# Local attention layer: taps taken in pairs, norms and reciprocals through 32x32 transposes, TensorE's order written out in nine turns

## The chip, the core and the metric

The kernel runs on one core of a Trainium2 chip. The metric is device time in microseconds (us); of a kernel's runs the median counts. Five engines work side by side, each on its own queue: TensorE (PE in the profile, its weight loads PEld) multiplies matrices into PSUM, VectorE (DVE), ScalarE (ACT) and GpSimd (POOL) work element by element, SyncE (SP) issues the DMAs. A queue is worked off in order: an instruction that waits holds up everything behind it on its engine.

## What is computed

Four residual layers, one after the other, on two images of 512 channels by 64x64 tokens, all in float32. The change is in layer 0, which is worked through once for each image. Cut to what matters:

```python
q = (xf @ W_q + b_q).reshape(B, N, nh, hd).transpose(0, 2, 1, 3)      # 8 heads of 64 channels
q_norm = _l2norm(q)
q_scaled = (q_norm + query_embedding[None]) * jax.nn.softplus(temperature)[None]
kv = xf @ W_kv + b_kv                                                 # k also divided by its norm
patches = ...                                                         # the 3x3 neighbours of a token
attn_local = jnp.einsum('bhnd,bhndk->bhnk', q_scaled, k_local)        # 9 "taps" per token and head
...
attn_pool = jnp.einsum('bhnd,bhpd->bhnp', q_scaled, _l2norm(k_pool))  # 256 pooled keys
attn = jax.nn.softmax(jnp.concatenate([attn_local, attn_pool], axis=-1), axis=-1)
a_local, a_pool = (attn[..., :ll], attn[..., ll:])
lt = jnp.einsum('bhnd,hdk->bhnk', q_norm, learnable_tokens) + learnable_bias[None] + a_local
x_local = jnp.einsum('bhnk,bhndk->bhnd', lt, v_local)
x_pool = jnp.einsum('bhnp,bhpd->bhnd', a_pool, v_pool)
out = ((x_local + x_pool).transpose(0, 2, 1, 3).reshape(B, N, C)) @ W_proj + b_proj
```

## The kernel before

**Units and turns.** Class `Local` holds the layer. Channels lie on the 128 partitions, so a chunk of 128 channels is two heads. A *unit* is one chunk with 1024 tokens (16 image rows); there are 4 chunks times 4 stretches of tokens, 16 units. The loop of `run` (from L1995) goes over *turns* i = -4 to 16, and in each turn works on several units at different stages: it projects k of unit i+4 and q of unit i+3 (and, from turn 3 on, v of unit i+1), divides the k and q that the turn before projected by their norms, makes the tap scores of unit i+1, does the softmax of unit i and weighs the values of unit i-1 with it. Turns 3 to 11 hold the same work; earlier and later ones hold less of one stage or another.

**Order.** Each stage is a Python generator. `in_turn` advances every stage by one `yield` after the other, so a turn has ten steps, and within a step the stages come in the order of the list `stages`: `norms`, `tap_products`, `attend`, `weigh`, `tap_sums`, `projections`, `normed`. This program order is where the framework starts; it then issues an engine's instructions in the order in which its own model of their durations finds them ready. That order is fixed at build time, and each engine follows it on the chip. Five of the eight PSUM banks are handed out by `bank()` to all stages, one more takes the tap sums, two take a copy of q.

**Norms.** `projections` leaves k or q of 512 tokens in SBUF (ACT, L2242) and its square in one of four tiles `sq` (ACT, L2244). A turn later `norms` multiplies four such squares by a matrix of ones (PE, L2276): the sum of squares of stream s and head r stands in row 32s + r of a bank. ACT copies the bank to `n_rows` (L2279), PE transposes it in four 128x128 pieces (L2283), so that the sums lie on tokens, and 13 small DVE operations of 32 elements (L2290 to L2298) make the inverse root: an integer first guess and three Newton rounds. The results go into `wide`, a tile of zeros, three yields later PE transposes it back (L2304) and ACT copies it (L2306). `normed` spreads each row over its 64 channels with a product (PE, L2318) and DVE multiplies k or q by it (L2326). `learned` then makes the scores of the learnable tokens (PE, L2339).

**Taps.** `tap_products` copies q into PSUM (ACT, L2361) and multiplies it by nine shifted windows of the image of k, one DVE operation of 1024 elements each (L2366), into three tiles in turn. `tap_sums` adds up the channels of each head with products of 32 columns (PE, L2379): tap k of half j goes to column group 2j + k % 2, so four of them can lie side by side in the array. ACT takes the exponential (L2394).

**Softmax.** `attend` makes the scores of the pooled keys in four pairs of products (PE, L2411) with their exponentials (ACT, L2415), multiplies them by the pooled values (PE, L2421), adds probabilities in pairs (POOL, L2426) and sums them (PE, L2433 and L2437) into a bank whose 32 rows of a group hold the two heads' denominators 16 times over, alternating. DVE takes the reciprocal of all 128x512 elements in two halves (L2458), and two more operations make the tap weights (L2461, L2462).

**Weighing.** The weights go through DRAM (SP, L2465) and come back spread over the partitions, one DMA pair for each of ten weights (`fetch_tap`, L2477), into a ring of three tiles. For each, `weigh` copies the tile into two banks (ACT, L2491), multiplies by the shifted v (DVE, L2496 and L2499) and adds to the output (POOL, L2504); when a tile is free again, the weight three further on is fetched. The sum goes to DRAM (SP, L2510). From turn 14 on `output` reads it back and multiplies by W_proj (PE, L2199), which `fetch_output` loads into the four `sq` tiles in turn 13 (L2175).

Of the kernel before, what the change touches and what calls it, by code (L numbers as in the profile page):

```python
# [3 lines left out]

# [1910 lines left out]
class Local:  # L1915
# [9 lines left out]
    def __init__(self, net, X, Y, sp_scale, d, wp, yp, pp, ppt, pps):  # L1925
        self.net, self.nc, self.vec, self.cst = net, net.nc, net.vec, net.cst
        self.X, self.Y, self.sp_scale, self.d = X, Y, sp_scale, d
        self.wp, self.pp, self.ppt, self.pps = wp, pp, ppt, pps
        nc, new = self.nc, lambda shape, name: wp.tile(shape, F32, name=name)

        self.yd = yp.tile([P, KC, N], F32, name="yd")
        self.wd = yp.tile([3, P, KC, C], F32, name="wd")
        self.rows = cycle([yp.tile([P // 2, self.UT], F32, name=f"rows{i}") for i in range(2)]).__next__

        R = W + 2
        flat = Y.rearrange("p k n -> p (k n)")
        self.next_w = flat[:, :KC * C].rearrange("p (kc o) -> p kc o", kc=KC)
        whole = Lent(flat)
        self.kx, self.vx = (whole.take([P, R, R]) for _ in range(2))
        qs, self.kraw = whole.take([P, 3 * self.UT]), whole.take([P, self.UT])  # L1940
        self.qs = [qs[:, i * self.UT:(i + 1) * self.UT] for i in range(3)]
        weighed = whole.take([P, 2 * self.UT])

        self.taps = ([weighed[:, i * self.UT:(i + 1) * self.UT] for i in range(2)]
                     + [new([P, self.UT], "tap2")])
        self.prods = [whole.take([P, self.UT])] + [new([P, self.UT], f"prod{i}") for i in range(2)]
# [19 lines left out]
        self.qn = new([P, self.UT], "qn")  # L1966
# [3 lines left out]
        self.wide = new([P, NT, P], "wide")  # L1970
# [12 lines left out]
        nc.gpsimd.memset(self.wide, 0.0)  # L1983

        nc.vector.tensor_tensor(self.qb, self.vec[:, V_QE:V_QE + KC], sp_scale, ALU.mult)

# [8 lines left out]
    def run(self):  # L1995
# [9 lines left out]
            self.fetch(i, 0)  # L2005
        for i in range(-4, units + 1):
            k, q, ahead, u, before = (unit(i + n) for n in (4, 3, 1, 0, -1))
            streams, ended = [], []
            stages = [self.norms(streams, ended)]
            if ahead is not None:  # L2010
# [4 lines left out]
                stages.append(self.weigh(before))  # L2015
            if ahead is not None:
                stages.append(self.tap_sums(ahead))

            values = ([ahead] if i >= self.UN - 1 and ahead is not None
                      else {-4: [0], -3: [1, 2], -2: [3]}.get(i, []))  # L2020
            stages.append(self.projections(k, q, values, streams))
# [4 lines left out]
                stages.append(self.fetch_output())  # L2026
            if i > units - 3:
                stages.append(self.output(i - units + 2))
            in_turn(*stages)

        self.nc.sync.dma_start(self.next_w, self.d["w_q1"].rearrange("(kc p) o -> p kc o", p=P))
        in_turn(self.output(KC - 1))
# [135 lines left out]

    def fetch_output(self):

        for _ in range(3):

            yield
        for kc in range(KC):
# [5 lines left out]
    def output(self, c4):  # L2180
# [1 line left out]

        nc, net = self.nc, self.net
        units = KC * self.UN
        toks = ([self.prods[0], self.prods[1], self.prods[2], self.qs[(units - 2) % 3]] if c4 % 2
                else [self.kraw, self.qn,
                      self.w3[:, :2].rearrange("p i k o -> p (i k o)"), self.qs[(units - 3) % 3]])
        for kc in range(KC):
# [43 lines left out]
    def projections(self, uk, uq, uvs, streams):  # L2232
# [19 lines left out]
        elif last - 1 in uvs:  # L2252

            uvs = [last - 1, last]
        values = [(u, j) for u in uvs for j in range(2)]
        for step in range(10):
            if step >= 6:
                project((uk, uq)[step // 2 - 3], "kq"[step // 2 - 3], step % 2)
            if step % 3 == 0 and values:
                u, j = values.pop(0)  # L2260
                self.value(u, j)
                if j and self.last(u):
                    self.fetch("v", u // self.UN + 1)
            yield

    def norms(self, streams, ended):
# [8 lines left out]
        for s in range(4):  # L2275
            nc.tensor.matmul(ps[32 * s:32 * s + 32, :], self.cst[:, C_E32:C_E32 + 32],  # L2276
                             before[s % len(before)][4], start=True, stop=True)
        rows = wp.tile([P, TB], F32, name="n_rows")
        nc.scalar.copy(rows, ps)  # L2279
        yield  # L2280
        ps = self.bank()
        for t in range(NT):
            nc.tensor.transpose(ps[:, t * P:(t + 1) * P], rows[:, t * P:(t + 1) * P],  # L2283
                                self.net.ident)


        sums = ps.rearrange("p (t s r) -> p t s r", t=NT, s=4)
        n, a = (sums[:, :, :, 2 * i:2 * i + 2] for i in range(2))
        y = wp.tile([P, NT, 4, 2], F32, name="roots")
# [4 lines left out]
        for i in range(3):  # L2294
            nc.vector.tensor_tensor(a, n, y, ALU.mult)
            nc.vector.tensor_tensor(a, a, y, ALU.mult)
            dst = self.wide.rearrange("p t (s r) -> p t s r", s=4)[:, :, :, :2] if i == 2 else y
            nc.vector.scalar_tensor_tensor(dst, a, 1.5, y, ALU.add, ALU.mult)  # L2298
        yield
        yield  # L2300
        yield
        ps = self.bank()
        for t in range(NT):
            nc.tensor.transpose(ps[:, t * P:(t + 1) * P], self.wide[:, t, :], self.net.ident)  # L2304
        rows = wp.tile([P, TB], F32, name="n_rows")
        nc.scalar.copy(rows, ps)  # L2306
        ended += [(s, rows[32 * s:32 * s + 2, :], *a) for s, a in enumerate(before)]
        yield

    def normed(self, ended):  # L2310

        nc = self.nc
        for _ in range(5):
            yield
        for which in "kq":
            mine = [(e, self.bank()) for e in ended if e[2] == which]
# [3 lines left out]
            for (_, _, _, u, j, part, _), ps in mine:  # L2320
                out = part
                if which == "k":
                    y = 1 + u % self.UN * self.UY + j * self.UY // 2
                    out = self.kx[:, y:y + self.UY // 2, 1:W + 1]
                    part, ps = (a.rearrange("p (y x) -> p y x", x=W) for a in (part, ps))
                nc.vector.tensor_tensor(out, part, ps, ALU.mult)  # L2326
            yield
        if mine:
            self.learned(mine[-1][0][3])
# [26 lines left out]
    def tap_products(self, u):  # L2356

        qs = self.pps.tile([P, self.UT], F32, name="qs")
        for j in range(2):
            part = slice(j * TB, (j + 1) * TB)  # L2360
            self.nc.scalar.copy(qs[:, part], self.qs[u % 3][:, part])  # L2361
        qs = qs.rearrange("p (y x) -> p y x", x=W)
        y = u % self.UN * self.UY
        for k in range(9):
            dy, dx = divmod(k, 3)
            self.nc.vector.tensor_tensor(  # L2366
                self.prods[k % 3].rearrange("p (y x) -> p y x", x=W), qs,
                self.kx[:, y + dy:y + dy + self.UY, dx:dx + W], ALU.mult)
            yield

    def tap_sums(self, u):

        nc = self.nc
        ps = self.ppt.tile([P, TB], F32, name="tap")

        def sums(k):
            for j in range(2):
                q = 2 * j + k % 2
                nc.tensor.matmul(ps[32 * q:32 * q + 32, :],  # L2379
                                 self.cst[:, C_TAPW + 16 - 2 * k:C_TAPW + 48 - 2 * k],  # L2380
                                 self.prods[k % 3][:, j * TB:(j + 1) * TB], start=(k < 2),
                                 stop=(k > 6))

        yield
        yield
        for k in range(0, 8, 2):
            sums(k)
            sums(k + 1)
            yield
            if k < 6:  # L2390
                yield
        sums(8)
        el = self.els()
        nc.scalar.activation(el, ps, AF.Exp)  # L2394
        self.el[u] = el
# [2 lines left out]
    def attend(self, u):  # L2398
# [43 lines left out]
        yield  # L2442
        exponentials(0, 1)
        yield
        values(0)
        yield
        exponentials(1, 0)
        yield
        exponentials(1, 1)
# [3 lines left out]
        yield  # L2453
        psD = sums()

        for i in range(2):
            part = slice(i * TB // 2, (i + 1) * TB // 2)
            nc.vector.reciprocal(self.recip[:, part], psD[:, part])  # L2458
# [242 lines left out]
```

## Time and profile before

| what | us |
|---|---|
| median of 3 runs (range) | 5152.03 (5151.96 to 5159.61) |
| the profiled execution's own time | 5163.61 |
| its span, first to last instruction | 5161.7 |
| TensorE busy | 4898.0 (95%) |
| VectorE busy | 3067.8 (59%) |
| ScalarE busy | 1863.1 (36%) |
| GpSimd busy | 1844.2 (36%) |
| mean granted TensorE clock | 0.979 of full speed |
| turns -3 to 0, first image | 194.6 to 326.9 |
| turns 1 and 2 | 326.9 to 419.7 |
| turns 3 to 11 | 419.7 to 818.2 |
| turns 12 and 13, then the tail with the output product | 818.2 to about 1000 |
| turns 3 to 11, second image | 2979.8 to 3378.6 |

A turn is bounded here by the first product of L2276, which every turn from -3 to 13 has. In the profile a line of instructions gives start, duration, engine, source line and operation, tiles written and read, and shape; "[2.21 <-PE mm L2318]" is idle time of the engine just before and who ended it. A matmul's duration overlaps the next one's, so what a product costs TensorE is read from start to start. A float32 product appears as two instructions.

### The profile page before, as it was taken

The numbers are of one execution on the slowest core, as the hardware profiler recorded it, in microseconds if no ns is written. First come the engines' busy times: TensorE is split into PE (matmuls) and PEld (weight loads), VectorE is DVE, ScalarE is ACT, GpSimd is POOL, SyncE is SP. The second block draws the span as 40 slices with busy tenths as digits, with TensorE's granted clock in tenths as the row PEclk, the third lists the DMA queues.
The fourth block names the chain that finished last, engine by engine and source line by source line (L and its number), as shares of the span: only waits on it lengthen the run. The fifth ranks groups of instructions, "written<-read, shape, count | busy, mean of one in ns | idle before, by whom it ended". The sixth has DMA issues, their size and how long they took to land. (4 is left out here: it accounts for less than half of the span.)

```text
span 5161.7 us, 48736 instructions
## 1 busy us (share of the span) xinstructions
PE 4898.0 (95%) x17299; PEld 2034.4 (39%) x17299; DVE 3067.8 (59%) x3986; ACT 1863.1 (36%) x3547; POOL 1844.2 (36%) x1216
## 2 busy tenths in 40 slices
PE   7999999899999999999999999998999999999998
PEld 3423332555334444433344333325543344444333
DVE  4266777644579633478732677776446795334766
ACT  1245565324323233322112555652343232333221
POOL 0035566500420045454500455555013201454554
PEclk9999999999999999999999999999999999999999
DMA  3025556600000000211110355565000000000111
GB/s 149 2 78 137 144 140 171 173 27 10 1 1 17 1 1 1 66 52 49 58 70 3 96 142 140 143 168 163 19 10 1 2 15 1 1 1 21 39 46 44
DMA packets 124752, 309.88 MB, mean 60 GB/s; under 512 B 20882, under 2 KB 33682, under 8 KB 122964
## 3 DMA queue, kind: packets, MB, share of 16 engines
q1 hardware_dynamic: 124500, 306.68, 21.0%
q8 instruction: 139, 2.28, 0.2%
q14 instruction: 113, 0.93, 0.1%
HBM read 258.11 MB, written 48.50 MB: 59 GB/s over the span
## 5 line engine op out<-in xcount | busy, mean ns | idle before, releaser
L134 PE MATMUL mm<-big,w 128*128 128x512 f32 x2496 | 1162.5, 610 | 9.2 <-DVE late L2458 9.2
L134 PEld LDWEIGHTS mm<-big,w 128*128 128x128 f32 x2496 | 455.9, 192 | 677.0 <-issue 559.0
L2504 POOL TENSOR_TENSOR late<-late,big 128x1024 f32<-128x1024 f32 x192 | 454.1, 2365 | 196.4 <-DVE big L2499 178.8
L1616 POOL TENSOR_TENSOR big<-big 128x512 f32<-128x512 f32 x224 | 277.3, 1270 | 219.8 <-ACT big L1607 219.8
L2426 POOL TENSOR_TENSOR late<-late 128x512 f32<-128x512 f32 x128 | 160.6, 1276 | 514.6 <-ACT late L2415 492.6
L2499 DVE TENSOR_TENSOR big<-big,mm 128x512 f32<-128x512 f32 x384 | 255.9, 683 | 124.5 <-ACT mm L2491 104.5
L2491 ACT COPY mm<-big 128x512 f32<-128x512 f32 x428 | 244.8, 593 | 174.0 <-DMA big<-rows 140.3
L1607 ACT ACTIVATE big<-mm,ed 128x256 f32<-128x256 f32 x512 | 193.6, 489 | 232.8 <-DVE top L1603 200.4
L2504 POOL TENSOR_TENSOR late<-late,tap 128x1024 f32<-128x1024 f32 x96 | 227.1, 2366 | 101.1 <-DVE tap L2499 97.8
L1420 POOL TENSOR_TENSOR wq<-prob 128x512 f32<-128x512 f32 x48 | 70.8, 1498 | 506.6 <-ACT prob L1417 506.6
L1871 PE MATMUL mm<-k,w 128*128 128x512 f32 x512 | 236.8, 606 | 12.3 <-DVE k L1864 7.3
L1603 DVE TENSOR_REDUCE top<-mm 128x1 f32<-128x512 f32 x256 | 159.1, 684 | 148.5 <-PE mm L1535 148.5
L134 PE MATMUL mm<-big,wq 128*128 128x512 f32 x512 | 235.2, 609 | 2.7 <-ACT off_t L1219 2.7
L2366 DVE TENSOR_TENSOR prod<-qs,big 128x1024 f32<-128x1024 f32 x192 | 230.7, 1217 | 8.7 <-PE tap L2379 7.0
L1191 PE MATMUL mm<-big,wo 128*128 128x512 f32 x512 | 234.7, 604 | 0.0
L1581 PE MATMUL mm<-w,big 128*128 128x512 f32 x512 | 234.5, 601 | 0.0
L1346 PE MATMUL acc<-big,diag 128*128 128x512 f32 x512 | 226.5, 601 | 4.6 <-ACT diag L1344 4.6
L1861 DVE RECIPROCAL psD<-psD 128x512 f32<-128x512 f32 x64 | 215.1, 3362 | 1.9
L969 POOL TENSOR_TENSOR group_stats<-group_stats,cst 128x1 f32<-128x1 f32 (+1 forms) x20 | 12.1, 621 | 570.2 <-DVE group_stats L968 538.7
L2379 PE MATMUL tap<-prod,cst 128*32 128x512 f32 x768 | 198.3, 602 | 8.9 <-DVE prod L2366 8.0
L134 PE MATMUL mm<-big,big 128*128 128x512 f32 x464 | 201.7, 594 | 0.5 <-DVE b_sr L1007 0.5
L1417 ACT ACTIVATE prob<-mm 128x512 f32<-128x512 f32 x256 | 133.0, 603 | 171.6 <-PE mm L1414 171.4
(410 smaller groups left out, 8477.2 us busy)
## 6 DMA issues: line engine op xcount, KB each, us to landing
big<-rows SPq DMA_DIRECT2D x428, 256.0 KB, 4.3
tap<-rows SPq DMA_DIRECT2D x212, 256.0 KB, 4.2
yd<-late SPq DMA_DIRECT2D x32, 512.0 KB, 2.9
lost_all<-lost SPq DMA_DIRECT2D x128, 128.0 KB, 3.1
out<-big SPq DMA_DIRECT2D x64, 256.0 KB, 2.0
big<-in_W_kv SPq DMA_DIRECT2D x8, 1024.0 KB, 9.4
rows<-late SPq DMA_DIRECT2D x64, 128.0 KB, 2.3
big<-yd SPq DMA_DIRECT2D x16, 512.0 KB, 5.1
```

Source lines behind the costliest of these rows:

```text
L134: self.nc.tensor.matmul(ps, w[:, kc, :], X[:, kc, blk * TB:(blk + 1) * TB], start=(kc == 0), stop=(kc == KC - 1))
L1191: nc.tensor.matmul(ps, w[:, kc, oc * P:(oc + 1) * P], att[:, kc, :], start=(kc == 0), stop=(kc == KC - 1))
L1346: nc.tensor.matmul(accs[b], dg, src[:, b * TB:(b + 1) * TB], start=(j == 0), stop=(j == 6))
L1581: nc.tensor.matmul(ps, X[:, kc, lo:lo + P], wv[:, kc, :], start=(kc == 0), stop=(kc == KC - 1))
L1616: nc.gpsimd.tensor_tensor(a, a, part, ALU.add)
L1861: nc.vector.reciprocal(psD, psD)
L1871: nc.tensor.matmul(ps, self.wo[:, kc, oc * P:(oc + 1) * P], qs[:, kc, :], start=(kc == 0), stop=(kc == KC - 1))
L2366: self.nc.vector.tensor_tensor(self.prods[k % 3].rearrange("p (y x) -> p y x", x=W), qs, self.kx[:, y + dy:y + dy + self.UY, dx:dx + W], A ...
L2379: nc.tensor.matmul(ps[32 * q:32 * q + 32, :], self.cst[:, C_TAPW + 16 - 2 * k:C_TAPW + 48 - 2 * k], self.prods[k % 3][:, j * TB:(j + 1) * ...
L2491: nc.scalar.copy(ps, part)
L2499: nc.vector.tensor_tensor(part.rearrange("p (y x) -> p y x", x=W), self.vx[:, y:y + self.UY // 2, dx:dx + W], ps.rearrange("p (y x) -> p y ...
L2504: nc.gpsimd.tensor_tensor(out, out, t, ALU.add)
```

## The change

- `tap_products` multiplies two taps with one operation of 2048 elements (the window of the second tap as a further dimension), and the ninth alone; the two product tiles hold two taps each, and a pair's four sums for each pass follow one another in `tap_sums`.
- `norms`: DVE transposes the bank of sums in place in blocks of 32x32, the 13 small operations work there, and a second 32x32 transpose writes the rows to `sq[3]`. Both copies by ACT and both sets of transposes by PE go, with `wide` and its clearing and with three yields.
- The reciprocal: DVE transposes the bank of denominators in place, takes the reciprocal of one of the 16 equal pairs (32 elements a partition), and transposes it, repeated 16 times, into `recip`.
- In turns 3 to 11 (`steady`) TensorE's instructions keep program order, and the steps are set anew: k is projected at steps 4 and 6, q at 7 and 8, v at 0 and 2; the norm rows are spread at steps 3 and 4; the first pooled values come one step later and in the same step as the next exponentials; the third pair of products is issued on DVE behind the multiplication of k by its inverse norms. In other turns the framework orders TensorE as before.
- `fetch_output` waits seven steps instead of three, `qn` and the product tiles change places in memory, and `output` reads the odd quarters into the four halves of the product tiles.

```diff
+            self.steady = self.UN <= i + 1 and i < units - 4
...
-            in_turn(*stages)
+            if self.steady:
+                with self.net.tc.manual_schedule(engines={mybir.EngineType.PE}):
+                    in_turn(*stages)
+            else:
+                in_turn(*stages)
...
-        for _ in range(3):
+        for _ in range(7):
...
+        made, taken = ((4, 6, 7, 8), (0, 2)) if self.steady else ((6, 7, 8, 9), (0, 3, 6, 9))
         for step in range(10):
-            if step >= 6:
-                project((uk, uq)[step // 2 - 3], "kq"[step // 2 - 3], step % 2)
-            if step % 3 == 0 and values:
+            if step in made:
+                i = made.index(step)
+                project((uk, uq)[i // 2], "kq"[i // 2], i % 2)
+            if step in taken and values:
...
-        rows = wp.tile([P, TB], F32, name="n_rows")
-        nc.scalar.copy(rows, ps)
-        yield
-        ps = self.bank()
-        for t in range(NT):
-            nc.tensor.transpose(ps[:, t * P:(t + 1) * P], rows[:, t * P:(t + 1) * P],
-                                self.net.ident)
+        yield
+        nc.vector.transpose(ps, ps)
...
-            dst = self.wide.rearrange("p t (s r) -> p t s r", s=4)[:, :, :, :2] if i == 2 else y
-            nc.vector.scalar_tensor_tensor(dst, a, 1.5, y, ALU.add, ALU.mult)
-        yield
-        yield
-        yield
-        ps = self.bank()
-        for t in range(NT):
-            nc.tensor.transpose(ps[:, t * P:(t + 1) * P], self.wide[:, t, :], self.net.ident)
-        rows = wp.tile([P, TB], F32, name="n_rows")
-        nc.scalar.copy(rows, ps)
+            nc.vector.scalar_tensor_tensor(n if i == 2 else y, a, 1.5, y, ALU.add, ALU.mult)
+        rows = self.sq[3]
+        nc.vector.transpose(rows, ps)
...
-        for _ in range(5):
+        for _ in range(3 if self.steady else 5):
             yield
...
+        for k in range(0, 9, 2):
+            n = min(2, 9 - k)
+            held = (self.net.tc.issue_after(self.multiplied) if self.steady and k == 4
+                    else nullcontext())
+            with held:
+                self.nc.vector.tensor_tensor(
+                    self.pair(u, k)[:, :n].rearrange("p k (y x) -> p k y x", x=W),
+                    bcast(qs.rearrange("p (y x) -> p y x", x=W), 1, n),
+                    self.shifted(u % self.UN * self.UY, k, n), ALU.mult)
+            yield
+            if n == 2:
+                yield
+
+    def pair(self, u, k):
+        return self.prods[(5 * u + k // 2) % 2]
...
+        for k in range(0, 9, 2):
+            for i in range(min(2, 9 - k)):
+                for j in range(2):
+                    q = 2 * j + i
+                    nc.tensor.matmul(ps[32 * q:32 * q + 32, :],
+                                     self.cst[:, C_TAPW + 16 - 2 * (k + i):][:, :32],
+                                     self.pair(u, k)[:, i, j * TB:(j + 1) * TB],
+                                     start=(k == 0), stop=(k + i > 6))
+            for _ in range(((2, 2, 3, 1, 0) if self.steady else (2, 2, 2, 1, 0))[k // 2]):
                 yield
...
+        if self.steady:
+            yield
         values(0)
-        yield
+        if not self.steady:
+            yield
         exponentials(1, 0)
...
-        for i in range(2):
-            part = slice(i * TB // 2, (i + 1) * TB // 2)
-            nc.vector.reciprocal(self.recip[:, part], psD[:, part])
+        nc.vector.transpose(psD, psD)
+        two = psD.rearrange("p (b n r) -> p b n r", n=16, r=2)[:, :, 0]
+        nc.vector.reciprocal(two, two)
+        nc.vector.transpose(self.recip.rearrange("p (b n r) -> p b n r", n=16, r=2),
+                            bcast(two, 2, 16))
```

More of the change, by code (lines that the diff above doesn't have):

```diff
@@ L1 @@
 import math
-from contextlib import ExitStack
+from contextlib import ExitStack, nullcontext
 from itertools import chain, cycle, islice
@@ L1945, in __init__ @@
                      + [new([P, self.UT], "tap2")])
-        self.prods = [whole.take([P, self.UT])] + [new([P, self.UT], f"prod{i}") for i in range(2)]
+        self.prods = [new([P, 2, self.UT], f"prods{i}") for i in range(2)]
         self.tok = whole.take([P, KC, 32])
@@ L1965, in __init__ @@
         self.vp = new([P, 2, C], "vp")
-        self.qn = new([P, self.UT], "qn")
+        self.qn = whole.take([P, self.UT])
         self.w3 = new([P, 3, KC, P], "w3")
@@ L1969, in __init__ @@
         self.half = new([P, 32], "mhalf32")
-        self.wide = new([P, NT, P], "wide")
         self.qb = new([P, KC], "qe_scaled")
@@ L1982, in __init__ @@
         nc.vector.memset(self.half, -0.5)
-        nc.gpsimd.memset(self.wide, 0.0)
         nc.vector.tensor_tensor(self.qb, self.vec[:, V_QE:V_QE + KC], sp_scale, ALU.mult)
@@ L2184, in output @@
         units = KC * self.UN
-        toks = ([self.prods[0], self.prods[1], self.prods[2], self.qs[(units - 2) % 3]] if c4 % 2
+        toks = ([a[:, i] for a in self.prods for i in range(2)] if c4 % 2
                 else [self.kraw, self.qn,
@@ L2277, in norms @@
                              before[s % len(before)][4], start=True, stop=True)
-        rows = wp.tile([P, TB], F32, name="n_rows")
-        nc.scalar.copy(rows, ps)
         yield
-        ps = self.bank()
-        for t in range(NT):
-            nc.tensor.transpose(ps[:, t * P:(t + 1) * P], rows[:, t * P:(t + 1) * P],
-                                self.net.ident)
-        sums = ps.rearrange("p (t s r) -> p t s r", t=NT, s=4)
-        n, a = (sums[:, :, :, 2 * i:2 * i + 2] for i in range(2))
-        y = wp.tile([P, NT, 4, 2], F32, name="roots")
+        nc.vector.transpose(ps, ps)
+        n, a = (ps.rearrange("p (b r) -> p b r", r=32)[:, :, 2 * i:2 * i + 2] for i in range(2))
+        y = wp.tile([P, TB // 32, 2], F32, name="roots")
         nc.vector.tensor_scalar(n, n, 1e-24, None, ALU.max)
@@ L2325, in normed @@
                     part, ps = (a.rearrange("p (y x) -> p y x", x=W) for a in (part, ps))
-                nc.vector.tensor_tensor(out, part, ps, ALU.mult)
+                self.multiplied = nc.vector.tensor_tensor(out, part, ps, ALU.mult).ins
+            yield
+        if self.steady:
             yield
@@ L2361, in tap_products, with shifted @@
             self.nc.scalar.copy(qs[:, part], self.qs[u % 3][:, part])
[L2362 to L2368, printed above, removed]
-            yield
+        for k in range(0, 9, 2):
[7 more added lines that the diff above has]
+                    self.shifted(u % self.UN * self.UY, k, n), ALU.mult)
+            yield
+            if n == 2:
+                yield
+    def pair(self, u, k):
+        return self.prods[(5 * u + k // 2) % 2]
+    def shifted(self, y, k, n):
+        a = self.kx[:, y:y + self.UY, :W]
+        at = lambda k: k // 3 * (W + 2) + k % 3
+        part, rows, cols = a.ap
+        return bass.AP(a.tensor, a.offset + at(k), [part, [at(k + 1) - at(k), n], rows, cols])
     def tap_sums(self, u):
@@ L2374, in tap_sums @@
         ps = self.ppt.tile([P, TB], F32, name="tap")
[L2376 to L2382, printed above, removed]
         yield
-        yield
-        for k in range(0, 8, 2):
-            sums(k)
-            sums(k + 1)
+        if not self.steady:
             yield
-            if k < 6:
+        for k in range(0, 9, 2):
[7 more added lines that the diff above has]
+            for _ in range(((2, 2, 3, 1, 0) if self.steady else (2, 2, 2, 1, 0))[k // 2]):
                 yield
-        sums(8)
         el = self.els()
@@ L2444, in attend @@
         yield
+        if self.steady:
+            yield
         values(0)
-        yield
+        if not self.steady:
+            yield
         exponentials(1, 0)
```

## The prediction

> **What bounds the kernel now.** I read the page's busy times first: TensorE is busy 95% of the span, no other engine over 59%. Then the windows by stage, with each engine's busy time in the part that the change touches: turns 1 and 2, turns 3 to 11 of the first image, and the same of the second.
>
> ```profile
> PE 4898.0 (95%) x17299; PEld 2034.4 (39%) x17299; DVE 3067.8 (59%) x3986; ACT 1863.1 (36%) x3547; POOL 1844.2 (36%) x1216
> ```
>
> ```profile
> core 0: us, PE busy (x) PEld busy (x) DVE busy (x) ACT busy (x) POOL busy (x), PEclk, DMA share, GB/s
> 326.90:419.70 92.80, 86.69 (x311) 26.62 (x306) 68.13 (x106) 52.48 (x93) 52.46 (x26) 0.98 0.52 139
> 419.70:818.20 398.50, 395.93 (x1437) 132.03 (x1436) 286.86 (x449) 241.27 (x423) 235.27 (x117) 1.00 0.55 141
> 2979.80:3378.60 398.80, 395.02 (x1441) 132.03 (x1441) 287.60 (x450) 241.28 (x423) 235.26 (x117) 1.00 0.55 141
> ```
>
> In the nine turns TensorE has 2.6 of 398.5 us idle, DVE 112. A turn takes (398.5 + 398.8) / 18 = 44.3 us, and TensorE's instructions set it: what is taken off its queue there comes off the time, until another loop is as long. In turns 1 and 2 it idles 6.1 of 92.8 us.
>
> Third, TensorE's timeline of one turn (start, duration, group), for the price of each group from start to start:
>
> ```profile
> 642.72 1.06 PE L2276 MATMUL mm<-sq,cst 128*32 128x512 f32 x8
> ...
> 645.76 0.66 PE L2283 MATMUL mm<-cst,n_rows 128*128 128x128 f32 x4
> 646.35 1.94 PE L2421 MATMUL mm<-late,vp 128*64 128x512 f32 x8
> ...
> 650.49 3.70 PE L134 MATMUL mm<-big,w 128*128 128x512 f32 x8
> 654.12 1.13 PE L2411 MATMUL mm<-big,kp 64*128 64x512 f32 x4
> ...
> 656.18 0.66 PE L2304 MATMUL mm<-cst,wide 128*128 128x128 f32 x4
> 656.76 1.94 PE L2421 MATMUL mm<-late,vp 128*64 128x512 f32 x8
> 659.11 1.13 PE L2318 MATMUL mm<-n_rows,cst 2*128 2x512 f32 x4 [0.41 <-ACT n_rows L2306]
> ```
>
> The two sets of transposes take 0.59 and 0.58 us, and the norm rows then wait 0.41 us for an ACT copy. The tap products come in six groups (at 644.77, 649.49, 655.18, 672.25, 681.33 and 682.2): nine taps that become ready one by one do not fill five.
>
> **The change, part by part.** Turns 3 to 11 first, 18 in all.
>
> *TensorE.* Transposes: 0.59 + 0.58 = 1.17 us less. Taps: the six groups hold 5.78 us (their starts to the next group); four pairs and a single are five at 1.00 (649.49 to 650.49), so 0.8 less. What is left: six projections at 3.63 (650.49 to 654.12) 21.8; four score pairs at 1.06 (643.71 to 644.77), 4.2; two value products at 1.87 (646.35 to 648.22), 3.7; two norm rows at 1.05 (659.11 to 660.16), 2.1; denominators (664.85 to 667.73) 2.9; taps 5.0; norm sums 1.0; learned scores 1.0. Sum 41.7 us against 44.3, so 2.6 less where nothing waits: 18 x 2.6 = 46 us.
>
> *DVE.* No row shows a plain 32x32 transpose. Ends: 0.2 us (a 32-element operation of the norm chain) and 3.4 us (both halves of L2458, the dearest 512 elements here). I take 0.69, the third row below, which transposes 512 elements on its way into a sum.
>
> ```profile
> L2366 DVE TENSOR_TENSOR prod<-qs,big 128x1024 f32<-128x1024 f32 x192 | 230.7, 1217 | 8.7 <-PE tap L2379 7.0
> ...
> L2458 DVE RECIPROCAL late<-mm 128x256 f32<-128x256 f32 x64 | 107.8, 1725 | 16.2 <-PE mm L2437 16.0
> ...
> L1799 DVE TRANSPOSE_TENSOR_REDUCE sq_cols<-sq 128x16 f32<-128x512 f32 x64 | 43.9, 694 | 26.8 <-POOL sq L1504 26.0 <-PE mm L1810 0.7
> ```
>
> A turn adds four transposes, 2.8, and a reciprocal of 32 elements (between 0.19 and 1.73; a quarter microsecond by its share of L2458 plus the small operation's 0.19: 0.4), and drops 3.4 of reciprocals. Pairs: consecutive products start 1.14 us apart (682.43, 683.57), operations of 512 elements 0.60 apart, so 0.06 is fixed and four pairs save 0.25. Net about -0.4 of 31.9 us a turn: a cover of ten idle microseconds. At the upper end DVE gains 10.8 us a turn, would need 42.3, and be the bound itself.
>
> *ACT and POOL.* Two copies (0.58 each) and the clearing of `wide` go; both engines have 15 idle microseconds a turn, so nothing on the path.
>
> *Waits that the fixed order adds.* Everything on TensorE queues behind a waiting product, so I compare TensorE's own work between producer and user with what must fit in. Norm rows (step 3): 9.4 us behind the sums of step 1; the chain is two transposes and 13 operations 0.235 apart (654.09 to 654.33), 4.4 us, and if DVE puts a pair of taps (2.2) and six weighings (3.6) in between, 10.2: a wait of 0 to 0.8. Denominators (step 7): 5.5 us after the second pooled values, against two POOL additions of 1.28 and one L2504 of 2.37 under way, 4.9: 0, or 1.7 if one more is ahead. Taps: a pair has over 3.5 us. Banks: five, with up to eight asked for in step 3, and 0.6 to 1.2 us of ACT or DVE to free one. Bounds 0 to 2.5 us a turn together; below nothing there is no gain, since the 41.7 holds no idle time. I take 0.5, nearer to what the same stages show now (0.3). Steady turns: 42.2 us, 18 x 2.1 = 37 us less.
>
> *Turns -3 to 2, 12 and 13* (16 in all) keep the framework's order. Transposes: 16 x 1.17 = 18.7, of which turns 1 and 2 count half, because TensorE waits for DVE there: 16. Before turn 3, TensorE's waits on the norm chain (L2283, L2304 and L2318, the view of waits) are 8 us an image; it loses two ACT copies and two crossings of engines and gains 1.4 us on DVE: a quarter, 4 us for both. Taps: 0.8 in seven turns each, a third of it, since some of these turns wait for DVE: 4. Sum 24, bounds 10 and 38.
>
> *The tail.* `output` reads its odd quarters into product tiles that are free since turn 14, where one had been a tile of q: nothing. The last units' denominators come 1.5 us sooner on DVE, twice: 3 us. W_proj: four steps later, behind a wait for `sq[3]`; its four DMAs land 4.5 us after issue and the first user starts at 908.6, some 20 us on. SP holds up the reload of `yd` and the tap fetches behind it if that cover is gone: 4.5 + 4 x 0.6 = 7 us an image, which I leave in the range.
>
> Sum: 37 + 24 + 3 = 64 us. The profiled execution took 5163.6 us with a span of 5161.7; it lies 0.2% over the median, and I take the difference from the median: **5152 - 64 = 5088 us**.
>
> **The skill beside two rows.** The Trainium skill's page "TensorE: Matmul & The Clock Gate", Part 4, gives about 275 ns for one transpose of 128x128 in a kernel. The rows agree on a single duration (273 ns), but four together hold the queue only 0.59 us. By the page, eight would free 2.2 us a turn and my sum would be some 32 us larger; by the rows 1.17. The page "TensorEngine Tiling (Array Packing)", Key Properties, says that a change of tiling mode drains TensorE, which speaks against an order that alternates forms. The rows price it: two projections in a row take 7.06 us, two apart 7.26, so 0.2 for one change more; the turn has about as many changes after (23) as before (24), and the sum stays.
>
> **Rivals.**
>
> *The ring of weights becomes the bound.* In the turn at 642 weighing begins at 642.0 (ACT), its sum goes out at 679.63 (SP), the next unit's first weight is fetched behind it on SP at 680.46 and copied at 685.55:
>
> ```profile
> 674.12 1.10 SPq L2465 DMA_DIRECT2D rows<-late  x2
> 679.63 0.33 SPq L2510 DMA_DIRECT2D yd<-late  x1
> 680.46 1.11 SPq L2477 DMA_DIRECT2D tap<-rows  x2
> ```
>
> That is a loop of 43.55 us, almost the turn. For the forecast: POOL stands idle 4.71 us in it (before 674.82), waiting for DVE, which is at reciprocals and tap weights, so it can shrink to about 39 to 42. Against: denominators now follow the second k and the learned scores, so weights land 2 to 4 us into the next turn. If the loop gives only 0.3 us, turns take 43.3: 18 + 24 + 3 = 45, **5107** (5097 to 5128).
>
> *Nothing waits.* The nine turns give all 46, the others 38, the tail 6: 90, **5062** (5050 to 5075). For it: 12 us of idle DVE a turn. Against: five banks.
>
> *Slower: the denominators wait on POOL.* With the order fixed, a product at step 7 holds all projections behind it. POOL has to do both additions after the second values, but follows its own order; if four weighing additions (2.37 each) stand ahead of them, the wait is 4 x 2.37 + 2.55 - 5.5 = 6.5 us a turn: 18 x 6.5 - 46 - 27 = +44, **5196**. It decides from (46 + 27) / 18 = 4.1 us a turn. Against: today its weight loads wait 1.9 us for POOL in the whole kernel.
>
> *It does not do what it says.* If a 32x32 transpose costs near the upper end, DVE takes TensorE's place at 44 us a turn, and what is left is part of the other turns: about **5145**.
>
> **How the numbers follow.** Forecast 0.50 (5075 to 5097), ring 0.25, nothing waits 0.13, no net effect 0.05, slower 0.07. A measurement of this kernel tells about 0.2% from no change, 10 us: the first three are faster, 0.88; same 0.05; slower 0.07. The range takes the first three nearly whole: 5054 to 5130.
>
> **What would show it.** Right: nine turns of 42.2 us (about 380 in each image), no L2283, L2304 or ACT copies of rows, five tap groups of 1.0, DVE transposes of about 0.69, DVE near 31.5 us a turn. Wrong: turns of 43 and more with weighing waiting for its DMA (ring); PE idle before the denominators with POOL named (slower); transposes of 1.5 us and more, and TensorE waiting for taps (DVE). I am most likely wrong in the waits of the fixed order, and in what turns 1, 2 and the tail give back.

## The result and the profile after

The changed kernel is slower: 5172.64 us median of 16 runs (5160.06 to 5183.75) against 5157.02 for the kernel before (16 runs beside them), ratio 1.0033, 95% interval 1.0024 to 1.0042. The forecast was 5088, the range 5054 to 5130. The profiled execution has a span of 5172.2 us against 5161.7, at nearly the same mean clock (0.977 and 0.979), so the difference is in the work.

The line of busy times of the changed kernel:

```profile
PE 4870.5 (94%) x17027; PEld 2006.9 (39%) x17027; DVE 3086.2 (60%) x3958; ACT 1827.2 (35%) x3479; POOL 1844.3 (36%) x1214
```

The windows of turns 3 to 11 of both images, in the columns of the same view of before:

```profile
418.30:828.40 410.10, 391.80 (x1385) 122.18 (x1384) 301.47 (x444) 232.05 (x407) 235.92 (x117) 0.99 0.53 139
2990.50:3398.80 408.30, 390.40 (x1388) 121.99 (x1387) 302.15 (x445) 232.24 (x407) 235.87 (x117) 1.00 0.52 140
```

TensorE has 272 instructions fewer in all, as intended, and is 27.5 us less busy. But nine turns take 410.1 and 408.3 us instead of 398.5 and 398.8: a turn is 45.5 us, not 42.2, and TensorE now stands idle for 18 us of nine turns, where it had 2.6. The nine turns lose 21 us in both images together; the rest of the two profiles gains 10.6, of it 10.3 in the other turns and the tail of this layer.

Where does TensorE wait? Its timeline in the fixed turn that starts at 555.20 (start, duration, group, idle time just before and who ended it):

```profile
556.19 1.12 PE L2411 MATMUL mm<-big,kp 64*128 64x512 f32 x2
558.19 1.12 PE L2411 MATMUL mm<-big,kp 64*128 64x512 f32 x2 [0.87 <-DVE late L2501]
...
560.93 4.65 PE L134 MATMUL mm<-big,w 128*128 128x512 f32 x8
565.51 1.94 PE L2421 MATMUL mm<-late,vp 128*64 128x512 f32 x8
```

The second pair of scores waits for L2501, the multiplication by weight 0, because it is given the bank in which that weight lies. Idle time is only part of it: the pair's products start 2.00 us apart (0.53 where nothing waits), and the projection behind them holds the queue 4.58 us from start to start instead of 3.63. The view of waits, for TensorE in nine turns of the first image (total, times, longest):

```profile
PE mm L2411 <- DVE late L2501: 7.0, 9, 1.8
PE mm L134 <- ACT late L2415: 4.8, 7, 1.4
PE mm L134 <- DVE big L2315: 4.7, 9, 0.5
```

For the kernel before, the same view holds 2.4 us in all. Why is weight 0 late? SP's queue in the changed kernel: the tap weights go out at 548.90 and weight 0 is asked for at 551.89; the weighed sum of the unit before follows it.

```profile
548.90 1.10 SPq L2470 DMA_DIRECT2D rows<-late  x2
551.89 1.11 SPq L2482 DMA_DIRECT2D tap<-rows  x2
...
554.79 0.33 SPq L2515 DMA_DIRECT2D yd<-late  x1
```

ScalarE's copy of it into the bank starts at 556.82, 1.6 us into the next turn, after 4.01 us idle for the DMA, with the exponentials of the new turn queued behind:

```profile
556.82 1.11 ACT L2496 COPY mm<-tap 128x512 f32<-128x512 f32 x2 [4.01 <-DMA tap<-rows]
```

This is a loop from turn to turn: denominators (L2437), tap weights on VectorE, rows to DRAM and back, weight 0, its bank, TensorE's fixed order, denominators. One of its links is new and dear. VectorE's groups of the nine turns (duration of one in ns at the end, then idle time):

```profile
L2358 DVE TENSOR_TENSOR prods<-qs,big 128x2048 f32<-128x2048 f32 x37 | 84.3, 2282 | 0.0
...
L2466 DVE TENSOR_TENSOR late<-late 128x512 f32<-128x512 f32 x9 | 21.6, 2396 | 0.3
...
L2459 DVE STREAM_TRANSPOSE mm<-mm 128x512 f32<-128x512 f32 x9 | 6.6, 732 | 0.0
...
L2461 DVE RECIPROCAL mm<-mm 128x32 f32<-128x32 f32 x9 | 3.2, 359 | 0.0
```

The transposes (0.73) and the small reciprocal (0.36) cost what was forecast. L2466, the unchanged multiplication of exponentials by reciprocals, takes 2.40 us; as L2461 of before it took 0.68. The two timelines, VectorE's and then GpSimd's, show what it meets:

```profile
545.01 0.70 DVE L2462 STREAM_TRANSPOSE late<-mm 128x512 f32<-128x512 f32 x1
545.75 2.40 DVE L2466 TENSOR_TENSOR late<-late 128x512 f32<-128x512 f32 x1
548.18 0.69 DVE L2467 TENSOR_TENSOR late<-late 128x512 f32<-128x512 f32 x1
```

```profile
545.23 2.37 POOL L2509 TENSOR_TENSOR late<-late,big 128x1024 f32<-128x1024 f32 x1 [1.34 <-DVE big L2504]
```

GpSimd's addition runs from 545.23 to 547.60; L2466 starts within it and ends 0.55 us after it. L2467 reads two SBUF tiles too and takes 0.69 with no addition under way. The Trainium skill's page "SBUF — State Buffer", section "Who interferes with whom", says that a VectorE instruction with two inputs in SBUF contends with a GpSimd instruction that reads SBUF, and that the one that came later is blocked. The trace agrees: 2.40 against 0.69 us.

### The profile page after: what moved, and what is told of

Its sections match the earlier page's. It is cut to its first block, busy times and chain, and to the rows that moved or that the text cites. A ratio compares the mean times of both kernels' runs of the same rounds, so it can differ in the third digit from the quotient of the medians.

```text
span 5172.2 us, 48018 instructions
## 1 busy us (share of the span) xinstructions
PE 4870.5 (94%) x17027; PEld 2006.9 (39%) x17027; DVE 3086.2 (60%) x3958; ACT 1827.2 (35%) x3479; POOL 1844.3 (36%) x1214
## 5 line engine op out<-in xcount | busy, mean ns | idle before, releaser
L134 PE MATMUL mm<-big,w 128*128 128x512 f32 x2496 | 1186.3, 619 | 35.8 <-ACT late L2415 11.2
L2358 DVE TENSOR_TENSOR prods<-qs,big 128x2048 f32<-128x2048 f32 (+1 forms) x160 | 329.5, 2068 | 35.3 <-PE tap L2387 24.8
L2387 PE MATMUL tap<-prods,cst 128*32 128x512 f32 x1152 | 192.1, 610 | 27.0 <-DVE prods L2358 26.9
```

Source lines behind the costliest of these rows:

```text
L134: self.nc.tensor.matmul(ps, w[:, kc, :], X[:, kc, blk * TB:(blk + 1) * TB], start=(kc == 0), stop=(kc == KC - 1))
L2358: self.nc.vector.tensor_tensor(self.pair(u, k)[:, :n].rearrange("p k (y x) -> p k y x", x=W), bcast(qs.rearrange("p (y x) -> p y x", x=W), ...
```

## The experiments

Theory A: the loop sets the turn, and the change makes it longer than TensorE's shortened work. Theory B, the main rival: TensorE's waits are local (transposes, the fixed order, banks), and the length of the loop does not matter. All kernels but e4, which ran once, were timed several times against the kernel before on the same chip. For the nine turns of both images the profiles give, in us: the mean turn, and as medians the place of the denominators (L2437 and its counterparts) in it; from them to the rows' issue; from there to the multiplication by weight 0; and that one's place, counted from the start of the same turn. "Split" is pairs made by two operations.

| kernel | ratio to before (95%) | turn | denominators at | to rows | to weight 0 | weight 0 at |
|---|---|---|---|---|---|---|
| before | 1 | 44.3 | 23.9 | 7.4 | 11.9 | 43.4 |
| e8 reciprocals twice | 1.0157 (1.0142 to 1.0172) | 46.5 | 24.1 | 10.1 | 10.8 | 45.2 |
| e5 new reciprocals | 1.0009 (1.0000 to 1.0018) | 44.5 | 24.3 | 6.9 | 9.0 | 40.3 |
| e6 and new norms | 0.9975 (0.9963 to 0.9986) | 44.1 | 23.9 | 6.9 | 9.0 | 39.8 |
| e2 and pairs | 1.0070 (1.0056 to 1.0084) | 46.4 | 23.5 | 9.6 | 11.7 | 45.0 |
| e11 as e2, split | 0.9951 (0.9933 to 0.9969) | 43.9 | 23.4 | 7.5 | 8.7 | 39.6 |
| after (fixed order) | 1.0033 (1.0024 to 1.0042) | 45.5 | 29.5 | 8.2 | 8.5 | 47.1 |
| e1 its steps, order free | 1.0095 (1.0079 to 1.0111) | 47.9 | 29.3 | 8.3 | 8.5 | 46.0 |
| e12 as after, split | 1.0008 (0.9997 to 1.0019) | 45.3 | 29.5 | 8.2 | 8.5 | 46.5 |
| e9 as after, banks exchanged | 1.0057 (1.0042 to 1.0072) | 46.3 | 30.3 | 8.4 | 8.5 | 47.3 |
| e3 reciprocals in PSUM | 0.9998 (0.9987 to 1.0009) | 44.5 | 29.1 | 7.6 | 8.5 | 45.2 |
| e7 and product in PSUM | 0.9964 (0.9951 to 0.9978) | 43.7 | 28.0 | 6.5 | 8.5 | 43.5 |
| e10 as e7, banks exchanged | 1.0000 (0.9989 to 1.0011) | 44.4 | 28.7 | 6.6 | 8.6 | 44.2 |
| e13 as e7, split | 0.9938 (0.9920 to 0.9957) | 43.6 | 28.0 | 6.6 | 8.7 | 43.8 |

**The order alone, undone in two ways.** e1 leaves TensorE to the framework in all turns but keeps the new steps; e2 keeps the old steps and the framework's order everywhere.

```diff
-            if self.steady:
-                with self.net.tc.manual_schedule(engines={mybir.EngineType.PE}):
-                    in_turn(*stages)
-            else:
-                in_turn(*stages)
+            in_turn(*stages)
```

> All of the change, but TensorE's order in turns 3 to 11 is the framework's again (the new steps stay). Theory A (the fixed order puts the second pair of scores behind a bank that the weighing of the first weight holds, and that weight lands about 1.5 us into the turn, so turn, denominators, DRAM and weights close a loop of 45 us): TensorE does other products in the meantime, turns fall to 42.0 to 43.0 us, the nine turns to 378 to 387, the whole to 5100 to 5130. Theory B (DVE's and POOL's part of the change is the cost, whatever TensorE's order): turns stay at 44.5 to 45.5, the whole at 5160 to 5175.

```diff
-            self.steady = self.UN <= i + 1 and i < units - 4
+            self.steady = False
```

> Pairs of taps and 32x32 transposes alone: order and steps of the kernel before in all turns. Theory A: the products taken off TensorE show, turns of 42.0 to 43.0 us, the whole 5090 to 5125. Theory B: turns 44 to 45, the whole 5150 to 5170.

Measured: 5206.02 and 5194.04 us. Both are above every figure expected: my theory that the fixed order is what lengthens the loop fell, since without it the rest of the change is slower still. The other edits had to be looked at one by one. Why e1's steps need 47.9 us in the framework's order stays open; of TensorE's waits in nine turns the pairs of taps come first with 13.6 us, then the exponentials with 10.8, and weight 0 has 0.3.

**The collision.** e3 leaves the reciprocals in their PSUM bank, so that L2466's counterpart, L2465, reads one SBUF tile.

```diff
-        nc.vector.transpose(self.recip.rearrange("p (b n r) -> p b n r", n=16, r=2),
-                            bcast(two, 2, 16))
+        nc.vector.transpose(psD.rearrange("p (b n r) -> p b n r", n=16, r=2), bcast(two, 2, 16))
...
-        nc.vector.tensor_tensor(el, el, self.recip, ALU.mult)
+        nc.vector.tensor_tensor(el, el, psD, ALU.mult)
```

> The change, but the second transpose of the reciprocals writes to the PSUM bank, and the multiplication reads it there, so it has one input in SBUF and not two. In the change this multiplication takes 2.40 us in turns 3 to 11, beside 0.69 where POOL does no addition. Theory A: it takes 0.69, the weights land 1.7 us sooner, a turn is 1.0 to 1.7 us shorter: the whole 5140 to 5155. Theory B in the form of too few banks: the bank is held 1.4 us longer and the time stays within 5165 to 5180.

Measured: 5154.59 us, as theory A has it, a turn of 44.5. Its groups in nine turns show the second half of the collision: the multiplication is cured, and the addition behind it, still with two SBUF tiles, now meets GpSimd.

```profile
L2466 DVE TENSOR_TENSOR late<-late 128x512 f32<-128x512 f32 x9 | 15.0, 1663 | 0.3
...
L2465 DVE TENSOR_TENSOR late<-late,mm 128x512 f32<-128x512 f32 x9 | 6.2, 687 | 0.3
```

**Is it the loop?** e4 cuts it: each unit is weighed with the weights of the unit before (so its output is another; the rows get four tiles in DRAM instead of two), and nothing in a turn waits for that turn's tap weights.

```diff
...
-        self.spread = self.rows()
+        new = self.rows()
...
+        self.spread, self.newest = getattr(self, "newest", new), new
```

> The change, but each unit is weighed with the weights of the unit before it (the first with its own), which have been in DRAM for a whole turn: all instructions stay, the output is another one, and the way from denominators to weights no longer ties one turn to the next. Theory A: TensorE no longer waits for the bank of the first weighing (L2501 in the change), turns of 41.7 to 42.7 us, the nine turns 375 to 384, one time of 5095 to 5125. Theory of too few banks: waits of 3 us a turn stay, nine turns above 400.

Measured, once: 5110.15 us. Nine turns take 384.9 and 383.9 us, 42.7 a turn, with the same instructions and L2466 still dear, and of TensorE's waits L2315 with 4.9 us and L2415 with 1.6 us in nine turns are left. The window of the first image, in the columns used above:

```profile
417.50:802.40 384.90, 378.42 (x1376) 118.92 (x1372) 298.38 (x442) 229.71 (x406) 236.00 (x118) 1.00 0.53 146
```

The turn of e4 that starts at 584.62 has TensorE's groups in the same order as the turn of the changed kernel shown above. From the second pair of scores to the first pooled values it takes 5.93 us (585.62 to 591.55), the changed kernel 9.32 (556.19 to 565.51). These 3.4 us are the whole difference between the two turns, 42.55 and 45.93 us: it arises where weight 0 is late. So the loop is worth 2.8 of the 3.8 us a turn that exceed the forecast's 41.7; another 0.7 are the two waits, and less than 0.3 is left.

The opposite test on the kernel before, e8, does its reciprocals twice.

```diff
-        for i in range(2):
+        for i in (0, 1, 0, 1):
             part = slice(i * TB // 2, (i + 1) * TB // 2)
```

> The kernel before with its two reciprocals done twice (the result is the same): VectorE has 3.4 us more a turn, all of it between denominators and tap weights. Theory A: the loop grows from about 43.5 to 46.9 us and becomes the turn: 18 x 2.6 = 47 more, and up to 10 in the other turns, 5195 to 5220 us. Theory B (VectorE's 12 idle us a turn take it, TensorE's work sets the turn): 5150 to 5170.

Measured: 5236.04 us, more than theory A expected. The rows go out 2.7 us later after the denominators and the turn grows by 2.2, though VectorE still has over ten idle microseconds in it (319.65 busy of 418.20). So what follows the denominators on VectorE had almost no room before. That it is the same loop isn't shown: of TensorE's waits in e8 the view names tap products (L2366, 4.2 us in nine turns) and ScalarE (L2244 and L2423, 6.3), not weight 0, and the fetch of weight 0 stands behind the weighed sum on SP there (more on this below). The windows of nine turns give 39 of the profile's 62 us; the rest is mostly in turn 12 and the tail.

**One edit after the other, order free.** e5 changes the reciprocals of the kernel before alone; e6 adds the norms; e2 above adds the pairs.

```diff
-        for i in range(2):
-            part = slice(i * TB // 2, (i + 1) * TB // 2)
-            nc.vector.reciprocal(self.recip[:, part], psD[:, part])
+        nc.vector.transpose(psD, psD)
...
```

> The kernel before with the reciprocal through 32x32 transposes as the only edit; norms, taps and the order of TensorE stay as they were. Theory A (a turn is set by the longer of TensorE's work, 44.0 us, and the loop denominators, tap weights, DRAM, first weighing, bank, scores, denominators, about 43.5 us): the loop becomes some 2 us shorter (3.4 us of reciprocals against 0.73 + 0.36 + 0.72), TensorE's work stays, so almost nothing: 5143 to 5158 us, turns of 43.9 to 44.4 us. Theory B (the transposes themselves, or the multiplication behind them beside a GpSimd addition, cost the time): slower than before by 10 us and more, 5165 to 5185.

> The kernel before with reciprocals and norms through 32x32 transposes, taps one by one as before, TensorE ordered by the framework in all turns. It differs from the run with all steps old (5194 us) by the pairs of taps alone. Theory A: TensorE loses 1.17 us a turn, the loop is near 41.5 us, so turns come to about 43.0: 18 x 1.2 = 22 less and a few us from the other turns, 5115 to 5140; what then separates it from 5194 is the pairs, 2.28 us operations in front of the tap weights on VectorE. Theory B (the norm chain on VectorE, 4.4 us in one piece, delays the tap weights as much as pairs do): near the run with old steps, 5175 to 5200.

Measured: 5162.93 and 5142.35 us (before, beside them: 5154.72). e5 lies between the two expectations: the loop got shorter (weight 0 at 40.3 instead of 43.4, most of it by another order on SP's queue, see below) and nothing was won, since TensorE is then busy all the time (0.07 us idle a turn; its tap groups take 6.6 us instead of 5.8). e6 is close to A's range; its turn fell by 0.2 against before and not by 1.2, because single taps that are ready at other times make tap groups of 6.8 us instead of 5.8. The step to e2, 52 us, belongs to the pairs and to what came with them. e11 tells what in them: the same tiles and the same groups on TensorE, but two VectorE operations for a pair.

```diff
-                self.nc.vector.tensor_tensor(
-                    self.pair(u, k)[:, :n]...,
+                for i in range(n):
+                    self.nc.vector.tensor_tensor(
+                        self.pair(u, k)[:, i:i + 1]...,
```

> The run with all steps old and TensorE ordered by the framework (5194 us), with each pair of taps made by two VectorE operations of 1024 elements into the same pair tile. Against the run with recips and norms (5142 us) it keeps the pair tiles and the pair groups on TensorE. Theory A (single operations of 2.28 us in front of the tap weights lengthen the loop): most of the 52 us come back, 5142 to 5165. Theory B (two tiles of pairs make VectorE and TensorE wait for each other, whatever the length of an operation): 5180 to 5200.

Measured: 5128.89 us, 65 less than e2 and better than A's range. VectorE's timeline in e2, from behind the small reciprocal (681.25) to the last step of the tap weights:

```profile
682.16 2.29 DVE L2358 TENSOR_TENSOR prods<-qs,big 128x2048 f32<-128x2048 f32 x1 [0.55 <-ACT qs L2352]
684.37 0.70 DVE L2462 STREAM_TRANSPOSE late<-mm 128x512 f32<-128x512 f32 x1
...
685.58 0.67 DVE L2466 TENSOR_TENSOR late<-late 128x512 f32<-128x512 f32 x1
686.17 2.28 DVE L2358 TENSOR_TENSOR prods<-qs,big 128x2048 f32<-128x2048 f32 x1
688.37 0.68 DVE L2467 TENSOR_TENSOR late<-late 128x512 f32<-128x512 f32 x1
```

Two pairs stand among the links of the chain, L2462, L2466 and L2467. In e11 the first two places hold operations of 1.2 us:

```profile
615.98 1.23 DVE L2359 TENSOR_TENSOR prods<-qs,big 128x1024 f32<-128x1024 f32 x1 [0.55 <-ACT qs L2352]
617.12 0.71 DVE L2463 STREAM_TRANSPOSE late<-mm 128x512 f32<-128x512 f32 x1
617.75 1.19 DVE L2359 TENSOR_TENSOR prods<-qs,big 128x1024 f32<-128x1024 f32 x1
```

From denominators to rows the split takes 2.1 us out. The 3.0 us that weight 0 gains further on (11.7 to 8.7) lie on SP's queue. In e2, and then in e11:

```profile
689.08 1.10 SPq L2470 DMA_DIRECT2D rows<-late  x2
694.63 0.33 SPq L2515 DMA_DIRECT2D yd<-late  x1
695.42 1.10 SPq L2482 DMA_DIRECT2D tap<-rows  x2
```

```profile
620.76 1.11 SPq L2471 DMA_DIRECT2D rows<-late  x2
623.80 1.10 SPq L2483 DMA_DIRECT2D big<-rows  x2
```

In e2 the weighed sum of the unit before stands ahead of weight 0's fetch, in e11 behind it. The framework fixes this order at build time, and it came out in two ways: in the kernel before, e8 and e2 the sum is first in all 18 turns, and the fetch is issued 6.0, 5.2 and 6.0 us after the rows; in all others of the table the fetch is first, 3.0 us after the rows, which have then just landed (2.9). A third thing changes with the split: in e2 the pairs themselves are TensorE's longest wait (L2387 for L2358, 14.0 us in nine turns), in e11 no tap is waited for. So the 65 us are those of longer operations together with the order that the build made of them; what the links of the chain, SP's order and the wait for pairs are worth each isn't shown.

**In the fixed order.** e7 keeps the product in PSUM as well:

```diff
-        nc.vector.tensor_tensor(el, el, psD, ALU.mult)
-        nc.vector.tensor_tensor(el, el, self.lt.pop(u), ALU.add)
+        nc.vector.tensor_tensor(psD, el, psD, ALU.mult)
+        nc.vector.tensor_tensor(el, psD, self.lt.pop(u), ALU.add)
```

> The kernel with reciprocals left in PSUM (5154.6 us), and the product with the exponentials written to PSUM as well, so that neither of the two operations that make the tap weights has two SBUF inputs. Theory A (the loop sets the turn, and an operation with two SBUF inputs waits for a GpSimd addition under way): the second operation falls from 1.66 to about 0.7 us, the turn from 44.5 to 43.6 us: 18 x 0.9 = 16 less, 5134 to 5146. Theory B (only the first of the two mattered, or TensorE's waits for banks do not depend on the weights): as before that edit, 5150 to 5160.

Measured: 5142.37 us, as A has it. Both operations take 0.69 to 0.70 us now. The addition in the same nine turns:

```profile
L2466 DVE TENSOR_TENSOR late<-mm,late 128x512 f32<-128x512 f32 x9 | 6.2, 692 | 0.3
```

Down the table from after to e3 to e7 the rows come 0.7 and 1.1 us sooner behind the denominators, and the turn falls by 1.0 and 0.8.

e9 and e10 let the first v product ask for its bank before weight 0 does, in the changed kernel and in e7.

```diff
+            if self.steady:
+                stages.append(self.first_value(ahead))
             if before is not None:
                 stages.append(self.weigh(before))
```

> The changed kernel, but in turns 3 to 11 the first v product of a turn asks for its PSUM bank before weight 0 does, not after it. TensorE's order stays the same; banks are handed out in a ring of five, so the second pair of scores takes over the v product's bank and not the one in which weight 0 is multiplied. Theory A (the loop closes through this bank): TensorE's waits of L2411 for VectorE's L2501, 7.0 us in nine turns and more in the weight loads, go; turns of 45.5 us fall by 0.8 to 2 us, 18 x that: 5136 to 5160 us. Theory B (the loop closes elsewhere as well, over ScalarE, whose copies of weights stand ahead of exponentials): the wait moves to the next product that needs an exponential, 5165 to 5180.

> The kernel with reciprocals and product in PSUM (5142.4 us) and the same exchange of banks. Theory A: its turns are 42.5 us where weight 0 comes in time and 43.8 to 47 where it does not; without the bank in the loop nearly all are near 42.5 to 43: 18 x 0.8 = 14 less, 5120 to 5136. Theory B (as for the exchange alone): 5138 to 5148.

Measured: 5186.79 and 5154.96 us, slower than without (1.0057 against 1.0033, and 1.0000 against 0.9964); both theories missed. In e9 the scores still wait for weight 0 (3.8 us in nine turns), so the banks do not go round as I had assumed, and a v product now takes over the bank in which VectorE works on the norms:

```profile
PE mm L134 <- DVE mm L2300: 6.6, 6, 1.4
```

In e10 no score waits for weight 0 any more, and the same L2300 holds TensorE up for 6.3 us.

So the bank of weight 0 is not the only one that holds TensorE up. In these two runs another late one came next, and through which of bank, ScalarE's queue and program order the loop would close in a better arrangement stays open.

e12 and e13 split the pairs, by the same edit as e11, in the changed kernel and in e7.

> The changed kernel, with its fixed order and steps in turns 3 to 11, and each pair of taps made by two VectorE operations of 1024 elements. Theory A (in the fixed turns the tap weights are not behind a pair of taps, but behind a GpSimd addition, a weighing multiplication and late denominators; in the other turns they are behind pairs): the nine turns stay at 45 to 45.6 us, turns 1 and 2 fall by about 3 us an image, 5155 to 5172 us. Theory B (the 2.28 us operations cost the same 65 us in the fixed order): turns near 43.9 us, 5115 to 5145.

> The kernel with reciprocals and product in PSUM (5142.4 us), fixed order in turns 3 to 11, and the pairs split in the same way. Theory A: 43.7 us turns as before the split, some us less in turns 1 to 3, 5128 to 5140 us. Theory B: turns near 42.5 us and less, 5105 to 5125.

Measured: 5153.78 and 5118.98 us. In both, the nine turns hardly move (45.5 to 45.3, 43.7 to 43.6): there the tap weights do not stand behind pairs, as A says. The time goes mostly from the turns before: turns 1 and 2 of the first image take 87.3 us in e13, 94.2 in e7. That was more than A's numbers for both runs; e13 even lies in B's range, but its turns are those of A. e13 is the fastest of all, ratio 0.9938 to the kernel before, and 0.9938 / 1.0033 = 0.9905 to the changed one. Its window for turns 1 and 2 of the first image:

```profile
324.00:411.30 87.30, 80.05 (x277) 25.19 (x273) 63.23 (x108) 50.21 (x89) 52.26 (x26) 0.96 0.53 141
```

## Why the prediction was wrong

- **TensorE's work, 41.7 us a turn: right.** The turn at 639.30 in e7 takes 42.55 us, with waits of 0.17 and 0.53 in it: 41.85. With the loop cut, e4 has 42.7.
- **VectorE's prices: right.** 0.70 to 0.73 for a transpose (0.69 taken), 0.36 for the reciprocal (0.4), 2.28 for a pair (2.2).
- **"Waits that the fixed order adds", 0.5 within 0 to 2.5: the step that failed.** It came to 45.5 - 41.7 = 3.8 us a turn, 18 x 3.3 = 59 us over. The step compared each product with its own producer, stage by stage, and never followed the way round from the denominators to the next turn's scores; with that way cut, 1.0 of the 3.8 is left (e4). Nor is the fixed order the source: without it the new steps need 47.9 us a turn (e1).
- **The ring as a rival: near it, but another loop, and its length misread.** The ring came round through the weighed sum, with the next weight 0 fetched behind it on SP. So it is in the kernel before; in the changed one the fetch (551.89) stands ahead of the sum (554.79) and waits for the rows, so the loop goes through denominators and tap weights. And 43.55 us is the time from one copy of weight 0 to the next, which comes out near a turn whatever sets the turn; it says nothing of the room in the ring. The same paragraph had the link that counts, weights that land 2 to 4 us into the next turn (it was 1.6), and let it cost at most 1.1 us a turn. The new steps move the denominators from 23.9 to 27.6 at the earliest. By a rough estimate that leaves 42 - 27.6 = 14.4 us for the rest of a loop that needs 15.0 even in e7 (6.5 + 8.5), and 16.7 in the changed kernel.
- **An edit costed at nothing: the multiplication by the reciprocals.** Its line is unchanged, and I let it be. With the new steps it starts inside a GpSimd addition, in all 18 turns: 1.7 us a turn on the loop. Taking the collisions away (e3 and e7) brought 1.8 us a turn, and from 1.0033 to 0.9964. The row of before, 0.68 us, showed only that no addition had run beside it there.
- **Pairs: "four pairs save 0.25" on VectorE was the wrong question.** An operation of twice the length makes whatever is queued behind it wait longer. In the changed kernel that costs 0.25% (1.0033 to 1.0008, e12), mostly outside the fixed turns; in the framework's order everywhere it costs 65 us, with the other order on SP that came with it (e2 and e11).
- **The other turns: -24 forecast with -3 in the tail, -10 measured together.** From the first norm sums to turn 3 the profiles give 6.9 us less in both images, from turn 12 to the last output product 3.4 (that product ends at 1068.8 in the first image of before, so the tail is longer than the table of before has it). With the pairs split, e12 gives 20.5 + 9.5 = 30 us, so the gain was there, and the pairs took two thirds of it back.
- **The other rivals.** Denominators waiting on GpSimd: the view of waits of nine turns names no GpSimd line for TensorE's products. Dear transposes: no, 0.70 to 0.73 us. The range ended at 5130 because the slower side held one mechanism alone, with 0.07; the loop's length was not let past 43.6 us.

## What to carry to other kernels

When work is taken off an engine that is busy all the time, first measure the loops that come back to it from one turn to the next, by adding up their links and not by the time from one pass to the next: their length has to be below the new turn, with the moved steps in it. Read the order of each queue anew after every edit, the DMA queue's too: here one build put a sum ahead of the fetch on the loop, 3 us, and another did not. An operation made twice as long to save its fixed cost delays everything that is queued behind it; look what on that queue lies on a loop. Where an operation with two SBUF inputs lies on a loop beside a busy GpSimd, give one of its inputs to PSUM.

## What the runs showed of the hardware

A VectorE operation with two SBUF inputs that starts inside a GpSimd addition of 2.37 us takes 2.40 us and ends 0.55 us after it (the changed kernel); one that starts 1.26 us into the addition takes 1.66 and ends the same 0.55 us after it (e3). With one input in PSUM it takes 0.69 beside the same addition (e3, e7). 32x32 transposes of 128x512 float32 elements out of PSUM take 0.70 to 0.73 us whether they write to PSUM or SBUF, and one that reads each pair of columns 16 times over (L2462) is no dearer, at 0.70.
